# A two-layer graph network on 64 graphs: the order of work at both ends, and the engine of one sum of spectra

## The chip, the cores and the metric

The kernel runs on one core of a Trainium2 chip. Its time is in device microseconds, and the figure for a kernel is the median of its runs. The kernel before has three: 2018.05, 2020.08 and 2021.51 us, median 2020.08.

The engines are named as in the profile: PE is the matrix engine (TensorE) and PEld its loads of weights, DVE is VectorE, ACT is ScalarE, POOL is GpSimd, and SP is the engine that issues most of the DMAs. All times are in microseconds; L12 is line 12 of the kernel before, unless the text says otherwise.

## The reference

The inputs are x and adj, both 64 graphs x 256 x 256 in float32. Cut to what matters here, `reference()` computes:

```python
# layer 0
deg = adj.sum(-1); deg = where(deg != 0, deg, 1)
a_plus = deg**-.5 * adj * deg**-.5 + max(alpha, 1e-10) * eye(256)
x = layernorm(x + (a_plus @ x) @ W.T + b)
# layer 1
h = relu(bn1(conv1(x)))                   # 1x1 convolution, 256 -> 256
x_conv = relu(bn2(conv2(h)) + x)          # 17 taps, 256 -> 256
s = x @ w_se.T + b_se                     # 3 numbers for each node
A = exp(-squared_distances(s)) * adj
x_nmp = A @ relu(x @ w_msg.T + b_msg)
gi = concat(x_conv, x_nmp) @ w_ih.T + b_ih; gh = x @ w_hh.T + b_hh
r, z = sigmoid(gi_r + gh_r), sigmoid(gi_z + gh_z)
out = layernorm(x + (1 - z) * tanh(gi_n + r * gh_n) + z * x)
```

## The kernel before, in words

**The whole.** Everything is in float32. The 64 graphs are worked in four quarters of 16. The convolution with 17 taps is done through a small Fourier transform along the nodes: the forward transform of each graph's h is p_dft (L538), the products with the spectra of the weights are p_k (L605), once a quarter for its 16 graphs, and the gates are p_g (L950), which take the largest part of PE's time. The spectra of the weights are made in 13 parts (`weights(n)`, NPARTS = 13), each beside one of the first graphs.

**What sets the order.** Each stage is a Python generator that yields between its pieces, and the code that interleaves them puts the pieces in a written order. A scheduler then orders the instructions of each engine; `tc.issue_after(op)` keeps an instruction from standing ahead of `op` in that order. Within an engine, instructions run in their order, so one that waits holds all behind it. GpSimd, SP and ACT also issue DMAs, in the same queues as their other work.

**Layer 0 of a graph g** (`layer0(g)`): ACT sums the rows of adj to degrees (L402); GpSimd raises them to the power -0.5 (`dis`, L412, named POWERS[g]); PE transposes adj in four blocks (p_adjT, L423); ACT copies the blocks to adjT; VectorE adds the diagonal, one L426 for each half (DIAGONAL[g]); ACT scales x by `dis` (L441, X_SCALED[g]); GpSimd adds the bias to x (L444, 128x512); PE makes p_hT (L449, 8 products); ACT copies it to hT (L454); PE makes p_out (in the bank p_out0, L459, 8 products); VectorE adds x to it (L464, two). The layer norm follows: statistics on VectorE (L355 to L357), a power on GpSimd (L358), the mean's product on VectorE (L362), and the scaling on ACT (L366, two). ACT then issues the store of x1 (L470).

**Layer 1 of a graph**, as far as it is spoken of here: PE transposes x1 (p_x1T, L484), does conv1 and the three columns of s together (p_conv, L499), the messages (p_msg, L520), the transform (p_dft, L538), the rows for the distances (p_rows, L551), the distances (p_dist, L561) and the aggregation (p_nmp, L574). VectorE squares the columns of s (`sq`, L509; L511 and L512 write `scols`, which p_rows reads). ACT relus the messages (L524).

**The first microseconds.** Two graphs (`firsts`) go through layer 0 beside the setup. SP's queue holds, in order, adj and x of graph 0, adj of graph 1, small vectors, x of graph 1 and weights. `batch_norms()` transposes the vectors of both batch norms (p_bn, L181), makes six diagonal matrices on VectorE (into VM, L195), and multiplies them by a matrix of ones (p_norm, L200) so that each vector stands in all 128 rows; these scale conv1 (wc, L204 and L207) and the taps. `without_first()` (L155) is a GpSimd subtraction of a row from a weight: once for wc, once for wmsg. `tables()` writes a period of a cosine (memsets, L234), copies 30 strided rows of it into `fwd_row` on VectorE (15 at L252, 15 at L253), loads six slices of it into `fwd` (L263, on SP), then loads x of graph 2, makes `w_row` on VectorE (L269 to L274), loads it as `wt` (L280, L281) and from it makes the matrix `dft_w` (L288).

**A part of the spectra** (`weights(n)`): six loads of taps for the next part; products p_u (L332) of dft_w with the taps for i = 0 and 1, and copies of them on ACT (L335); after the second, VectorE scales the next part's taps (L316, for part 0 before all this); then VectorE takes the difference of the two spectra (L341, 120x1024), GpSimd their sum (L342, 120x1024), and GpSimd issues three stores `ud` (L344).

**The end.** `gru(63)` works its 128 top rows and its 128 lower rows apart, and the top rows in two halves of columns. After the products, `mixed()` makes tanh's input (L1007 to L1013), the gated x (L1016) and calls tanh; `rest()` (L927, L928) finishes a piece; `finished()` and `ended()` run `normed()`, a layer norm and a store (L921) issued by ACT. The top rows' second half of columns comes last:

```python
        mixed(top, slice(1, 2))
        nc.vector.bn_stats(st[:, 1, :], y[:, 0, HD:])
        NORMS.append(normed(g, top, y, st))
        ended()
```

Of the kernel before, what the change touches and what calls it, by code (L numbers as in the profile page):

```python
# [14 lines left out]
P = 128  # L15
# [11 lines left out]
def kernel(  # L27
# [100 lines left out]
    neg_half = const.tile([P, 4], F32)  # L128
    nc.vector.memset(neg_half, -0.5)
    load(0)  # L130
    nc.scalar.dma_start(alpha_t, bcast_rows(alpha, 1))
# [44 lines left out]
    def batch_norms(pool):  # L176


        scale = pool.tile([P, D], F32, name="scale")
        p = bank("p_bn")  # L180
        nc.tensor.transpose(p[:, :16], vectors, ident[:16, :16])  # L181
        cols = pool.tile([P, 4, 4], F32, name="bn")
        nc.vector.tensor_copy(cols.rearrange("p i n -> p (i n)"), p[:, :16])
        g, b, m, v = (cols[:, i, :] for i in range(4))
        nc.vector.tensor_scalar(v, v, BN_EPS, None, op0=ALU.add)
        nc.gpsimd.tensor_tensor(v, v, neg_half, op=ALU.pow)
        ones = pool.tile([P, P], F32, name="ones")
        nc.vector.memset(ones, 1.0)
# [41 lines left out]
    def tables(pool):  # L230
# [18 lines left out]
        for n, f in enumerate(FREQ):  # L249

            if f < 0 or f % 3 == 0:
                nc.vector.tensor_copy(fwd_row[:, :, RE[n]], wave(f, False, FL))  # L252
                nc.vector.tensor_copy(fwd_row[:, :, IM[n]], wave(-f, True, FL))  # L253
# [38 lines left out]

    TAPS_OF, NORMALISED, STATISTICS = {}, [], []

# [23 lines left out]
    def weights(pool, n, scale):  # L318
# [4 lines left out]
        if n == 0:  # L323
            scaled(tp, scale)
        m = NU * GC
# [14 lines left out]
        with tc.issue_after(ADEG[n + 3]), tc.issue_after(POWERS[n + 3]):  # L340
            nc.vector.tensor_sub(us[3], us[1], us[0])  # L341
            nc.gpsimd.tensor_tensor(us[2], us[0], us[1], op=ALU.add)  # L342
# [4 lines left out]
    def layernorm(y, eps=LN_EPS, normed=None, parts=None, first=None):  # L347

# [12 lines left out]
        with tc.issue_after(ADEG[first]) if first in ADEG else ExitStack():  # L361
            nc.vector.scalar_tensor_tensor(mr[:, : len(chunks)], mv[:, : len(chunks), 0], -1.0, rs[:, : len(chunks)], op0=ALU.mult, op1=ALU.mult)  # L362
        if normed is not None:
            yield
        for c in chunks:
            op = nc.scalar.activation(  # L366
# [21 lines left out]
    EVICTED, RELU, SQUARED, AGGREGATED, LAYER0, POWERS = {}, {}, {}, {}, {}, {}  # L388
    ADJT, X1, X_SCALED, DIAGONAL, ADEG = {}, {}, {}, {}, {}


    def layer0(g):
# [13 lines left out]

        at = X_SCALED[0] if g == 1 else AGGREGATED.get(g - 3)
        with tc.issue_after(at) if at else ExitStack():
# [25 lines left out]

        if g > 1:
            yield
# [6 lines left out]
        with tc.issue_after(POWERS[max(g, 1)]):  # L443
            nc.gpsimd.tensor_tensor(x_t, x_t, b0_t.unsqueeze(1).to_broadcast([P, NCH, D]), op=ALU.add)  # L444
        hT = work.tile([P, DCH, N], F32, name="hT", bufs=1)
        p = bank("p_hT").rearrange("p (k n) -> p k n", k=DCH)
        for k in range(DCH):
            for mc in range(NCH):
                nc.tensor.matmul(  # L449
                    p[:, k, :], x1[:, mc, k * P : (k + 1) * P],  # L450
                    adjT[:, mc, 1 - mc : 3 - mc, :].rearrange("p n q -> p (n q)"),
                    start=mc == 0, stop=mc == NCH - 1,
                )
        nc.scalar.copy(hT, p)  # L454
        yield
        p = bank("p_out0").rearrange("p (c o) -> p c o", c=NCH)
        for c in range(NCH):
            for k in range(DCH):
                nc.tensor.matmul(  # L459
                    p[:, c, :], hT[:, k, c * P : (c + 1) * P], w0[:, k, :], start=k == 0, stop=k == DCH - 1  # L460
                )
        for c in range(NCH):
            mark(
# [454 lines left out]
    def normed(g, part, y, parts=None):  # L918

        yield from layernorm(y, 4 * LN_EPS, None, parts)  # L920
        nc.scalar.dma_start(out[g].rearrange("(c p) d -> p c d", p=P)[:, part], y)  # L921

    REST = []

    def rest():
        z, i, yq = REST.pop()
        nc.vector.scalar_tensor_tensor(i, z, 1.0, i, op0=ALU.subtract, op1=ALU.mult)  # L927
        nc.vector.tensor_sub(yq, yq, i)  # L928

# [4 lines left out]
    def gru(g):  # L934
# [68 lines left out]
        def mixed(part, cols=slice(0, 2)):  # L1003
# [8 lines left out]
            )  # L1012
            nc.vector.scalar_tensor_tensor(i, n, 0.5, i, op0=ALU.mult, op1=ALU.add)  # L1013
            y = x1[:, part]
# [20 lines left out]

        top = slice(0, 1)
        squashed(0, top)
# [114 lines left out]
    with tc.tile_pool(name="setup", bufs=1) as setup:  # L1152
# [236 lines left out]
```

## Time and profile before

| | before |
|---|---|
| median of 3 runs | 2020.08 (2018.05 to 2021.51) |
| the profiled execution's own time | 2018.59 |
| its span | 2016.8 |
| its mean granted TensorE clock | 0.997 |
| PE busy | 1977.2 (98%), 8169 matmuls |
| DVE busy | 1396.2 (69%), 3221 instructions |
| ACT busy | 970.4 (48%), 2310 instructions |
| POOL busy | 681.2 (34%), 651 instructions |
| HBM | 147 GB/s over the span |

The profile is of one execution, whose span starts with its first instruction and ends with its last; the time of that execution is 1.79 longer than its span. The slices that the page prints are 50.4 us each, so the first slice holds the setup, both first graphs and the start of the third. In a row of the timeline the first number is the start, the second how long the row's instructions took together from the first to the end of the last, and x8 how many they are; in brackets stands the idle time of the engine just ahead, and what ended it. A row of the windows has the stretch's length, then busy time and count of PE, of its weight loads, of DVE, ACT and POOL, then the granted clock, the busy share of the DMA engines, and GB/s.

### The profile page before, as it was taken

Reading aid. Unit: us, or ns where it says so; the run is one execution under the profiler, and the core shown is the slowest. Engines: PE = TensorE matmul, PEld = TensorE weight load, DVE = VectorE, ACT = ScalarE, POOL = GpSimd, SP = SyncE. Lnnn points to the kernel's source line nnn. Section 1 sums busy time; section 2 is a strip of 40 time slices with the busy share of each in tenths; the row PEclk is TensorE's granted clock in tenths of the full one; section 3 lists DMA queues with packets and bytes.
Section 4 is the critical chain, followed back from the end, with each engine's and each line's share of the span. In section 5 each row is a group of like instructions: output and inputs, shape, how many; then the busy total and the mean of one; then the engine's idle time right before and its main releaser. Section 6 shows DMA issues by size and latency. Waiting matters only on the chain.

```text
span 2016.8 us, 26474 instructions
## 1 busy us (share of the span) xinstructions
PE 1977.2 (98%) x8169; PEld 1439.2 (71%) x8169; DVE 1396.2 (69%) x3221; ACT 970.4 (48%) x2310; POOL 681.2 (34%) x651
## 2 busy tenths in 40 slices
PE   7999999999999999999999999999999999999998
PEld 6888788878677766777777766778878655555554
DVE  6344448787567788764446888874338899788887
ACT  5766654567442234566653233557762233333333
POOL 4444411132433243223322234231230344444543
PEclk9999999999999999999999999999999999999999
DMA  4676657544546744343335665434229554534331
GB/s 135 207 224 214 199 191 241 167 137 132 140 136 212 215 125 133 115 136 110 105 105 182 210 182 139 123 105 141 100 71 301 156 141 126 131 90 103 96 92 58
DMA packets 256803, 298.88 MB, mean 148 GB/s; under 512 B 70470, under 2 KB 199116, under 8 KB 256662
## 3 DMA queue, kind: packets, MB, share of 16 engines
q1 hardware_dynamic: 195798, 200.39, 33.7%
q10 hardware_dynamic: 44480, 67.39, 9.4%
q0 software_dynamic: 16384, 29.40, 6.5%
q8 instruction: 67, 1.10, 0.2%
q14 instruction: 74, 0.61, 0.1%
HBM read 193.97 MB, written 103.08 MB: 147 GB/s over the span
## 4 chain that ended last, share of the span: by engine, by line
PE 83%; DVE 11%; ACT 2%; issue 1%; DMA 1%; POOL 1%; ACTq 0%; POOLq 0%; DVEq 0%
PE p_g L950 36%; PE p_k L605 11%; PE p_hT L449 5%; PE p_out L459 5%; PE p_nmp L574 5%; PE p_conv L499 4%; PE p_msg L520 4%; PE p_dft L538 4%; PE p_u L332 2%; PE p_dist L561 2%; PE p_x1T L479 2%; PE p_adjT L423 1%; DMA u<-ud 1%; DVE ln_st L355 1%; PE p_xcT L898 1%
## 5 line engine op out<-in xcount | busy, mean ns | idle before, releaser
L950 PE MATMUL p_g<-wall,sums 128*128 128x384 f32 x1536 | 532.8, 487 | 1.7 <-DVE G L982 1.7
L950 PEld LDWEIGHTS p_g<-wall,sums 128*128 128x128 f32 x1536 | 285.4, 190 | 187.7 <-issue 8.2
L950 PE MATMUL p_g<-wall,inputs 128*128 128x384 f32 x1152 | 406.0, 488 | 3.7 <-DVE G L972 3.5
L950 PEld LDWEIGHTS p_g<-wall,inputs 128*128 128x128 f32 x1152 | 216.2, 190 | 156.5 <-DVE G L972 15.7
L358 POOL TENSOR_TENSOR ln_rs<-ln_rs,neg_half 128x2 f32<-128x2 f32 x129 | 97.1, 753 | 566.8 <-DVE ln_rs L357 430.2
L914 POOL TENSOR_TENSOR sums<-inputs 128x384 f32<-128x384 f32 x128 | 150.2, 1173 | 261.9 <-PE p_g L950 235.2
L565 DVE TENSOR_TENSOR aT<-aT,adjT 128x512 f32<-128x512 f32 x64 | 44.5, 696 | 202.6 <-ACT aT L562 202.4
L605 PE MATMUL p_k<-u,VM 128*128 128x256 f32 x736 | 169.8, 380 | 2.6 <-DMA u<-ud 1.4
L444 POOL TENSOR_TENSOR x_t<-x_t,b_t 128x512 f32<-128x512 f32 x64 | 101.9, 1592 | 204.9 <-ACT x L441 111.2
L605 PEld LDWEIGHTS p_k<-u,VM 128*128 128x128 f32 x736 | 138.9, 190 | 24.8 <-ACT ab L651 3.6
L366 ACT ACTIVATE x_g<-x_g,ln_mr,ln_rs 128x256 f32<-128x256 f32 x128 | 70.0, 593 | 156.8 <-DVE ln_mr L362 155.4
L1001 ACT ACTIVATE G<-G 128x512 f32<-128x512 f32 (+1 forms) x129 | 81.0, 628 | 125.9 <-DVE G L1030 87.7
L449 PE MATMUL p_hT<-adjT,x 128*128 128x256 f32 x512 | 125.2, 388 | 5.8 <-ACT x L441 2.6
L499 PE MATMUL p_conv<-wc,xn 128*128 128x259 f32 x512 | 124.8, 386 | 0.7 <-issue 0.7
L574 PE MATMUL p_nmp<-aT,msg 128*128 128x256 f32 x512 | 121.3, 380 | 1.9 <-DVE aT L565 1.9
L459 PE MATMUL p_out<-w,hT 128*128 128x256 f32 x512 | 121.4, 380 | 0.9 <-ACT hT L454 0.7
L974 ACT COPY G<-p_g 128x512 f32<-128x512 f32 x64 | 37.4, 585 | 174.4 <-PE p_g L950 116.2
L520 PE MATMUL p_msg<-wmsg,xn 128*128 128x256 f32 x512 | 121.3, 379 | 0.0
L914 POOL TENSOR_TENSOR sums<-inputs,sums 128x384 f32<-128x384 f32 x64 | 72.6, 1134 | 137.6 <-PE p_g L950 137.5
L538 PE MATMUL p_dft<-fwd,h 128*128 128x240 f32 x512 | 114.1, 366 | 0.0
L499 PEld LDWEIGHTS p_conv<-wc,xn 128*128 128x128 f32 x512 | 98.1, 192 | 21.3 <-issue 1.1
L449 PEld LDWEIGHTS p_hT<-adjT,x 128*128 128x128 f32 x512 | 93.9, 193 | 22.9 <-ACT x L441 7.1
(174 smaller groups left out, 3582.7 us busy)
## 6 DMA issues: line engine op xcount, KB each, us to landing
u<-ud SPq DMA_DIRECT2D x284, 256.0 KB
xn_d<-xn ACTq DMA_DIRECT2D x64, 512.0 KB
inputs<-xn_d SPq DMA_DIRECT2D x64, 512.0 KB
ud<-u_set POOLq DMA_DIRECT2D x39, 480.0 KB, 6.1
adj_t<-in_adj_dram SPq DMA_DIRECT2D x64, 256.0 KB
x_t<-in_x_dram SPq DMA_DIRECT2D x64, 256.0 KB
x_d<-x ACTq DMA_DIRECT2D x64, 256.0 KB
xc_d<-VM SPq DMA_DIRECT2D x64, 256.0 KB
```

What stands on the lines that cost most here:

```text
L358: nc.gpsimd.tensor_tensor(rs[:, : len(chunks)], rs[:, : len(chunks)], neg_half[:, : len(chunks)], op=ALU.pow)
L444: nc.gpsimd.tensor_tensor(x_t, x_t, b0_t.unsqueeze(1).to_broadcast([P, NCH, D]), op=ALU.add)
L449: nc.tensor.matmul(p[:, k, :], x1[:, mc, k * P : (k + 1) * P], adjT[:, mc, 1 - mc : 3 - mc, :].rearrange("p n q -> p (n q)"), start=mc == ...
L459: nc.tensor.matmul(p[:, c, :], hT[:, k, c * P : (c + 1) * P], w0[:, k, :], start=k == 0, stop=k == DCH - 1)
L499: CONV1[g] = nc.tensor.matmul(p, x1T[:, k, c * P : (c + 1) * P], wc1[:, k, :], start=k == 0, stop=k == DCH - 1).ins
L520: nc.tensor.matmul(p[:, c, :], x1T[:, k, c * P : (c + 1) * P], wmsg[:, k, :], start=k == 0, stop=k == DCH - 1)
L538: nc.tensor.matmul(p[:, t0 * FL : t1 * FL], h[:, c, k * P : (k + 1) * P], fwd[:, first : first + t1 - t0, :].rearrange("p t f -> p (t f)") ...
L574: nc.tensor.matmul(p[:, k, :], msg[:, mc, k * P : (k + 1) * P], aT[:, mc].rearrange("p n q -> p (n q)"), start=mc == 0, stop=mc == NCH - 1,)
L605: nc.tensor.matmul(p[:, j * D : (j + 1) * D], v[:, k, :], u[:, k, :], start=k == 0 and j == 0 and not onto, stop=k == DCH - 1, skip_group_ ...
L914: nc.gpsimd.tensor_tensor(S[i], x, y, op=op)
L950: nc.tensor.matmul(p[:, : 3 * HD] if k == 0 else p[:, HD:], a[:, k], wall[:, b, k].rearrange("p t d -> p (t d)"), start=first and k == 0, ...
L1001: nc.scalar.activation(rz, rz, AF.Tanh, scale=0.5)
```

## The change

- A matrix of ones is made first of all, and `awake(9)` issues nine 128x128 products of it with itself ahead of the first load's line; one more stands after the transposes of each of the two first graphs. Nothing reads their results.
- The two first graphs and `batch_norms` go in another order: hT of graph 0, out0 of graph 0, hT of graph 1, the norms' products p_norm, out0 of graph 1. New names (HT, OUT0, AGGREGATE, BIASED, MEANS) carry the constraints between them. The subtraction of wc stands behind the bias sum of graph 1's x.
- The 15 copies L253 go from VectorE to ACT, behind the scaled x of graph 1. The two operations that complete `fwd_row` stand behind the first statistics. Of SP's loads, x of graph 2 goes ahead of the six of `fwd`. The first part's taps are scaled behind graph 0's normalised x. The degrees of graph 2 stand behind it too.
- The last part's sum of spectra (L342 for n = 12) goes from GpSimd to VectorE.
- At the end the lower rows' layer norm is tied behind the top rows' tanh input (MIXED) and the rest of the norms behind the last finished piece (RESTED). The top rows' final scaling is split: the left half of the columns on ACT, the right half on VectorE, and two stores, the right half's by SP and the left half's by ACT.

```diff
+    ones = const.tile([P, P], F32, name="ones")
+    nc.vector.memset(ones, 1.0)
+    def awake(times):
+        p = bank("p_awake")
+        for _ in range(times):
+            nc.tensor.matmul(p[:, :P], ones, ones, start=True, stop=True)
+    awake(9)
     load(0)
...
             if f < 0 or f % 3 == 0:
                 nc.vector.tensor_copy(fwd_row[:, :, RE[n]], wave(f, False, FL))
-                nc.vector.tensor_copy(fwd_row[:, :, IM[n]], wave(-f, True, FL))
+        behind_diagonal.close()
+        yield
+        with tc.issue_after(X_SCALED[1]):
+            for n, f in enumerate(FREQ):
+                if f < 0 or f % 3 == 0:
+                    nc.scalar.copy(fwd_row[:, :, IM[n]], wave(-f, True, FL))
+        yield
+        behind_diagonal.enter_context(tc.issue_after(STATISTICS[0]))
...
         behind_diagonal.close()
+        load_x(2)
         for j in range(GT // 2 + 2):
             ...
             nc.sync.dma_start(fwd[lo:hi, j, :], fwd_row[:, lo - first : hi - first])
-        load_x(2)
...
         if n == 0:
-            scaled(tp, scale)
+            with tc.issue_after(NORMALISED[0]):
+                scaled(tp, scale)
...
-            nc.gpsimd.tensor_tensor(us[2], us[0], us[1], op=ALU.add)
+            (nc.gpsimd if n + 1 < NPARTS else nc.vector).tensor_tensor(us[2], us[0], us[1], op=ALU.add)
...
+        if halved:
+            nc.vector.tensor_scalar(
+                y[:, 0, D // 2 :], y[:, 0, D // 2 :], rs[:, 0:1], mr[:, 0:1], op0=ALU.mult, op1=ALU.add
+            )
+            nc.scalar.activation(
+                y[:, 0, : D // 2], y[:, 0, : D // 2], AF.Identity, bias=mr[:, 0:1], scale=rs[:, 0:1]
+            )
+            return
...
-        at = X_SCALED[0] if g == 1 else AGGREGATED.get(g - 3)
+        at = X_SCALED[0] if g == 1 else NORMED[0] if g == 2 else AGGREGATED.get(g - 3)
...
-        if g > 1:
+        if g > 0:
             yield
...
+            nc.sync.dma_start(to[:, :, HD:], y[:, :, HD:])
+            nc.scalar.dma_start(to[:, :, :HD], y[:, :, :HD])
...
-        finished(slice(1, 2), mixed(slice(1, 2)))
+        y1 = mixed(lower)
         nc.vector.tensor_add(quarter(0, 1), quarter(0, 1), p5)
-        squashed(0, slice(1, 2))
-        mixed(top, slice(1, 2))
+        squashed(0, lower)
+        mixed(top, lower)
+        with tc.issue_after(MIXED[0]):
+            finished(lower, y1)
         nc.vector.bn_stats(st[:, 1, :], y[:, 0, HD:])
-        NORMS.append(normed(g, top, y, st))
-        ended()
+        with tc.issue_after(RESTED[0]):
+            ended()
+        run(normed(g, top, y, st))
...
         for stage in firsts:
             next(stage)
+            awake(1)
         next(norms)
-        with tc.issue_after(POWERS[1]):
-            without_first(wc1, top[:, : D + NSE], nc.gpsimd)
-            nc.gpsimd.tensor_copy(wc1[0:1, 0, D:], biases[:, :NSE])
         load_adj(2)
         fill = tables(setup)
         next(fill)
-        for stage in firsts:
-            next(stage)
-        run(take(firsts[0], 2))
-        with tc.issue_after(STATISTICS[0]):
+        next(firsts[0])
+        with tc.issue_after(HT[0]):
             next(firsts[1])
+        next(fill)
+        next(firsts[0])
+        with tc.issue_after(OUT0[0]):
+            next(firsts[1])
+        with tc.issue_after(BIASED[1]):
+            without_first(wc1, top[:, : D + NSE], nc.gpsimd)
+            nc.gpsimd.tensor_copy(wc1[0:1, 0, D:], biases[:, :NSE])
+        with tc.issue_after(AGGREGATE[1]):
+            next(norms)
+        next(firsts[0])
+        next(fill)
+        run(firsts[0])
+        with tc.issue_after(MEANS[0]), tc.issue_after(HT[1]):
             scale2 = next(norms)
-        run(firsts[0])
+            next(firsts[1])
         run(fill)
```

More of the change, by code (lines that the diff above doesn't have):

```diff
@@ L186, in batch_norms @@
         nc.gpsimd.tensor_tensor(v, v, neg_half, op=ALU.pow)
-        ones = pool.tile([P, P], F32, name="ones")
-        nc.vector.memset(ones, 1.0)
         with tc.issue_after(DIAGONAL[1]):
@@ L252, in tables @@
                 nc.vector.tensor_copy(fwd_row[:, :, RE[n]], wave(f, False, FL))
-                nc.vector.tensor_copy(fwd_row[:, :, IM[n]], wave(-f, True, FL))
+        behind_diagonal.close()
[4 more added lines that the diff above has]
+                    nc.scalar.copy(fwd_row[:, :, IM[n]], wave(-f, True, FL))
+        yield
+        behind_diagonal.enter_context(tc.issue_after(STATISTICS[0]))
         parts = fwd_row[:, :, 16:].rearrange("p t (h n) -> p t h n", h=2)
@@ L291, in tables @@
         )
-    TAPS_OF, NORMALISED, STATISTICS = {}, [], []
+    TAPS_OF, NORMALISED, STATISTICS, MEANS = {}, [], [], {}
     def load_taps(pool, n):
@@ L345, in weights, with layernorm @@
         yield
-    def layernorm(y, eps=LN_EPS, normed=None, parts=None, first=None):
+    def layernorm(y, eps=LN_EPS, normed=None, parts=None, first=None, halved=False):
         chunks = range(y.shape[1])
@@ L361, in layernorm @@
         with tc.issue_after(ADEG[first]) if first in ADEG else ExitStack():
-            nc.vector.scalar_tensor_tensor(mr[:, : len(chunks)], mv[:, : len(chunks), 0], -1.0, rs[:, : len(chunks)], op0=ALU.mult, op1=ALU.mult)
+            mean = nc.vector.scalar_tensor_tensor(mr[:, : len(chunks)], mv[:, : len(chunks), 0], -1.0, rs[:, : len(chunks)], op0=ALU.mult, op1=ALU.mult)
+        MEANS.setdefault(0, mean.ins)
         if normed is not None:
             yield
+        if halved:
[6 more added lines that the diff above has]
+            return
         for c in chunks:
@@ L388 @@
     EVICTED, RELU, SQUARED, AGGREGATED, LAYER0, POWERS = {}, {}, {}, {}, {}, {}
-    ADJT, X1, X_SCALED, DIAGONAL, ADEG = {}, {}, {}, {}, {}
+    ADJT, X1, X_SCALED, DIAGONAL, ADEG, BIASED, HT, AGGREGATE, OUT0 = {}, {}, {}, {}, {}, {}, {}, {}, {}
     def layer0(g):
@@ L443, in layer0 @@
         with tc.issue_after(POWERS[max(g, 1)]):
-            nc.gpsimd.tensor_tensor(x_t, x_t, b0_t.unsqueeze(1).to_broadcast([P, NCH, D]), op=ALU.add)
+            BIASED[g] = nc.gpsimd.tensor_tensor(x_t, x_t, b0_t.unsqueeze(1).to_broadcast([P, NCH, D]), op=ALU.add).ins
         hT = work.tile([P, DCH, N], F32, name="hT", bufs=1)
@@ L448, in layer0 @@
             for mc in range(NCH):
-                nc.tensor.matmul(
+                AGGREGATE[g] = nc.tensor.matmul(
                     p[:, k, :], x1[:, mc, k * P : (k + 1) * P],
@@ L452, in layer0 @@
                     start=mc == 0, stop=mc == NCH - 1,
-                )
-        nc.scalar.copy(hT, p)
+                ).ins
+        HT[g] = nc.scalar.copy(hT, p).ins
         yield
@@ L458, in layer0 @@
             for k in range(DCH):
-                nc.tensor.matmul(
+                out0 = nc.tensor.matmul(
                     p[:, c, :], hT[:, k, c * P : (c + 1) * P], w0[:, k, :], start=k == 0, stop=k == DCH - 1
                 )
+        OUT0[g] = out0.ins
         for c in range(NCH):
@@ L918, in normed @@
     def normed(g, part, y, parts=None):
-        yield from layernorm(y, 4 * LN_EPS, None, parts)
-        nc.scalar.dma_start(out[g].rearrange("(c p) d -> p c d", p=P)[:, part], y)
-    REST = []
+        yield from layernorm(y, 4 * LN_EPS, None, parts, halved=parts is not None)
+        to = out[g].rearrange("(c p) d -> p c d", p=P)[:, part]
+        if parts is None:
+            nc.scalar.dma_start(to, y)
+        else:
+            nc.sync.dma_start(to[:, :, HD:], y[:, :, HD:])
+            nc.scalar.dma_start(to[:, :, :HD], y[:, :, :HD])
+    REST, MIXED, RESTED = [], {}, {}
     def rest():
@@ L927, in rest @@
         nc.vector.scalar_tensor_tensor(i, z, 1.0, i, op0=ALU.subtract, op1=ALU.mult)
-        nc.vector.tensor_sub(yq, yq, i)
+        RESTED[0] = nc.vector.tensor_sub(yq, yq, i).ins
     def ended():
@@ L1012, in mixed @@
             )
-            nc.vector.scalar_tensor_tensor(i, n, 0.5, i, op0=ALU.mult, op1=ALU.add)
+            MIXED[0] = nc.vector.scalar_tensor_tensor(i, n, 0.5, i, op0=ALU.mult, op1=ALU.add).ins
             y = x1[:, part]
@@ L1034, in gru @@
             return
-        top = slice(0, 1)
+        top, lower = slice(0, 1), slice(1, 2)
         squashed(0, top)
```

## The prediction

> **What bounds the kernel now.** I read the page first: where PE is not full, and who is on the chain that ended last.
>
> ```profile
> PE   7999999999999999999999999999999999999998
> ...
> PE 83%; DVE 11%; ACT 2%; issue 1%; DMA 1%; POOL 1%; ACTq 0%; POOLq 0%; DVEq 0%
> ```
>
> PE is the bound in every slice but the first and the last. An edit gains only where PE waits, or where it runs at half clock. So I went through the timeline of the first 34 us.
>
> ```profile
> 7.89 6.15 PE L449 MATMUL p_hT<-adjT,x 128*128 128x256 f32 x16
> ...
> 14.01 1.19 POOL L155 TENSOR_TENSOR wc<-wc,top 128x518 f32<-128x518 f32 x1 [3.88 <-DMA taps<-in_conv2T_dram]
> 14.04 1.22 DVE L252 COPY fwd_row<-period 1x48 f32<-1x48 f32 x1
> 15.16 1.26 POOL L444 TENSOR_TENSOR x_t<-x_t,b_t 128x512 f32<-128x512 f32 x1
> 15.18 1.31 DVE L253 COPY fwd_row<-period 1x48 f32<-1x48 f32 x1
> ...
> 21.47 1.27 POOL L155 TENSOR_TENSOR wmsg<-wmsg,top 128x512 f32<-128x512 f32 x1
> 22.00 0.75 DVE L362 SCALAR_TENSOR_TENSOR ln_mr<-ln_mv,ln_rs 128x2 f32<-128x2 f32 x1
> 22.79 1.09 ACT L366 ACTIVATE x<-x,ln_mr,ln_rs 128x256 f32<-128x256 f32 x2 [2.53 <-DVE ln_mr L362]
> ...
> 25.53 3.79 PE L499 MATMUL p_conv<-wc,xn 128*128 128x259 f32 x8 [0.70 <-issue]
> ...
> 33.52 1.89 PE L449 MATMUL p_hT<-adjT,x 128*128 128x256 f32 x8
> ```
>
> From p_conv at 25.53 PE is dense. A copy of 48 numbers normally follows the last by 0.11 us, but takes 1.2 to 1.3 beside a large GpSimd sum and ends with it; the 128x2 product L362 (0.15 elsewhere) is held to the end of the wmsg sum. One long GpSimd sum stops VectorE. Next the windows, for the clock:
>
> ```profile
> 19.70:23.10 3.40, 0.13 (x2) 0.00 (x0) 3.37 (x11) 0.70 (x2) 2.26 (x3) 1.00 0.06 8
> 23.10:26.50 3.40, 2.34 (x6) 1.52 (x7) 3.40 (x21) 2.87 (x9) 0.27 (x2) 0.50 0.48 121
> 26.50:29.90 3.40, 3.40 (x11) 2.69 (x10) 0.25 (x3) 0.98 (x5) 1.18 (x2) 0.50 0.16 47
> ...
> 2006.20:2009.60 3.40, 1.18 (x4) 0.38 (x2) 3.16 (x10) 1.46 (x3) 0.00 (x0) 1.00 0.24 80
> 2009.70:2013.00 3.30, 0.00 (x0) 0.00 (x0) 2.10 (x11) 0.91 (x2) 1.20 (x2) 0.50 0.01 3
> ```
>
> Second column: busy PE; third from the end: granted clock. The clock steps every 3.4 us: half after a stretch with 0.13 us of PE, full again after a full one, half after one with only 1.18. Before the first step no clock is recorded, but p_hT's 16 records in 6.15 us, against 8 in 1.89 later, show half speed at the start too. Last, graph 12, whose weights part is the last of 13:
>
> ```profile
> 233.81 2.96 POOL L342 TENSOR_TENSOR u_set<-u_set,u_set 120x1024 f32<-120x1024 f32 x1
> 234.49 2.31 DVE L509 SCALAR_TENSOR_TENSOR sq<-scols 128x6 f32<-128x6 f32 x1
> 237.11 2.69 DVE L426 SCALAR_TENSOR_TENSOR adjT<-ident,adeg,adjT 128x128 f32<-128x128 f32 x2
> 237.44 0.41 PE L551 MATMUL p_rows<-ident,scols 128*128 128x128 f32 x2 [0.56 <-DVE scols L512]
> 239.95 1.53 PE L449 MATMUL p_hT<-adjT,x 128*128 128x256 f32 x6 [1.67 <-DVE adjT L426]
> ```
>
> The GpSimd sum of spectra holds L509, the next x_t sum holds L426, and PE stands still. By the starts of its products (p_rows 0.72 after p_dft could hand over, p_hT 1.83) that is 2.55 us.
>
> **The change, part by part** (line numbers of before).
>
> Last sum on VectorE: the GpSimd sum of 2.96 goes; VectorE does it in about 1.21 (L341, same shape). By the new order: L341 233.35 to 234.56, L509 to 234.7, the sum to 235.85, L511, L426, L512 and L426 (0.16, 0.35, 0.26, 0.35, overlapping) to 236.65. PE wants p_rows at 236.72 and p_hT at 236.94; the x_t sum cannot start before ACT's scaled x at 236.69. So 2.5 comes back. If x_t's sum catches the second L426 first, 1.27 is lost again: bounds 1.2 to 2.55.
>
> First graph. GpSimd now does x_t's first bias sum ahead of wc's subtraction, from about 10.2 (the second `dis`, 9.44 + 0.70), to 11.5. That falls on VectorE's diagonals L195, which ran free at 10.24 to 11.6; one or two slip by, the next waits. GpSimd then waits for bn2_bias (`less_one`), does the second x_t sum at 12.7 to 14.0, and wc's subtraction at 14.0 to 15.2 as before, its load being the same. Both hold VectorE, so most of the 15 copies L252 run from 15.25: 15 x 0.114 = 1.7, to 17.0. (At half clock in hT the second sum is at 13.3 and the copies end at 17.1: the products of ones, nine of 0.43 at half clock = 3.8 us from 1.1, fill PE's wait for adj at 4.97 and cost nothing, but decide little.) L464 on x of graph 0 at 17.0 and 17.4, against 19.15 for the second one before; from there to the end of L357 was 1.55, so 18.95; L358 0.08 + 0.72, to 19.75; the wmsg sum directly behind it, 1.27, to 21.0, holds L362 as it did. ACT's L366 starts at 21.03 instead of 22.79: 1.75 gained. p_conv came 2.75 later: 23.8.
>
> Clock. From p_conv to p_hT of graph 2 the chain's own pieces give 1.75 + 0.44 + 1.73 + 1.62 + 0.22 = 5.76 at full clock; it took 7.99, so 2.2 went to the half clock. Now PE's last products before p_conv are p_out0 of graph 1, behind L464 at 17.9 to 19.8, and only the transposes at 21.7 stand in the 4 us to 23.8. The row of 2006.20 says that a third of a window does not hold the clock, so it falls about 22 to 25 and returns one full window (3.41) later: 1.0 to 2.7 lost, taken as 1.8. That is 0.4 gained. The Trainium skill, "TensorE: Matmul & The Clock Gate", Part 1, lets the clock fall only after an idle window; by it the first graph would stay at full clock and gain some 1.4 more, to 2014.5. The row at 2006.20, one third busy and then half clock, is against it.
>
> The gain has a cap. Graph 1's L464 comes behind wc (0.67 + 0.40) and w_row (1.2), at 23.3; 0.87 + 0.73 + taps 1.20 + 0.3 for statistics, two GpSimd powers of 0.70, L362: 28.1; then ACT: two L366 1.1, msg 0.6, scaled x 0.5 with issue between: p_hT of graph 2 not before 30.7, 2.8 before the 33.52 of now. Start: -2.1, bounds -0.5 and -2.8.
>
> Moved at no cost: 15 copies on ACT (its 128x4 copy 0.19, 1x256 0.36: about 3 us) in the 3.57 us it idled before the second hT; behind them waits that hT copy, and p_out0, which waits for L464 at 17.9 anyway. Uncovered they would cost 0.4. SP takes x of graph 2 at 17.5 instead of 23.74; the six `fwd` loads still start at 19.4 (19.29 before), and the last now stands behind the landing of ACT's x1 store. Behind it queue six `wt`, adj, x and seven `taps`. The store goes out at 22.2; the last output's, issued at 2013.87, had landed by 2015.61, so SP goes on at some 25, `fwd` is there at 27.7, p_dft comes at 29.4. Two spare ones products (0.43) lie in PE's waits for adj and bn.
>
> Graph 1. The first product of part 1 (p_u) moves from the adjT transposes into the middle of p_dft; taps' scaling L316 moves from 42.28 to behind L341 (44.36 to 45.58). There GpSimd's sum is already waiting (44.95) and takes over, as at 233.81: to 47.80. L316, two SBUF inputs, 1.22: to 49.05. PE is at p_u after conv, adjT, msg and half of p_dft: 43.38 + 1.75 + 0.44 + 1.73 + 0.81 = 48.1. So +1.0; zero if L316 wins the port, 1.2 at most.
>
> End. The operations left ahead of L1013, tanh's input, are 0.12 shorter in sum, so it comes that much sooner; but the lower rows' L362 now stands ahead of the top's aggregate and waits for GpSimd at 2011.8, so the top's mean is known at 13.15 instead of 13.2.
>
> ```profile
> 2013.24 0.60 ACT L366 ACTIVATE x_g<-x_g,ln_mr,ln_rs 128x256 f32<-128x256 f32 x1 [1.18 <-DVE ln_mr L362]
> 2013.87 0.35 ACTq L921 DMA_DIRECT2D out_dram<-x_g  x1
> ```
>
> Half of the row on ACT ends at 13.67 (0.48), the store of the lower rows is issued first (0.37), so the last store starts at 14.1, not 13.87: +0.2; bounds -0.2 (smaller store) and +0.5 (three stores at once).
>
> Sum: -2.1 - 2.5 + 1.0 + 0.2 = -3.4. The profiled execution took 2018.59 (span 2016.8): 2015.2. The median of the runs, 2020.08, lies 1.5 above that execution; half of it is added, since four executions spread over 3.5 us: 2015.9, that is 0.21% under the median. About 0.2% is what a measurement of this kernel can tell from no change; the border lies at 2016.0.
>
> **Rivals.** *Ports lie more kindly*: VectorE gets the pair between sums, L316 does not wait, the start reaches its cap: -2.8 - 2.5 + 0 + 0.2 = -5.1, 2014.2. For it: at 16.40 copies got through between two sums. Against: every L342 that met waiting work won.
>
> *Part of it comes back*: x_t's sum holds L426 at graph 12 (-1.2) and the start gives 0.8: -0.8 - 1.2 + 1.0 + 0.2 = -0.8, 2018.5. For it: 1.5 us of start are three estimates long.
>
> *Slower*: SP behind the x1 store. From a landing later than 26.6 p_dft waits (29.4 less issue and landing, 2.7) us for us; past 34 the loss passes 3.4 + 4 and the kernel is slower by over 0.2%, some 2025. Against it: 1.74 for a store in the row above.
>
> *It does not do what it says*: nine products do not raise the clock before hT. Then hT of graph 0 stays at 3.8 us; by the working above this moves L464 by 0.1, 2016.0. It is counted in the first case.
>
> **How the numbers follow.** Forecast 0.45 (own range 2014.6 to 2017.4, somewhat over half of it under 2016.0, 0.27), kind ports 0.18, part comes back 0.25, slower 0.12. Faster 0.27 + 0.18 = 0.45; same 0.18 + 0.25 = 0.43; slower 0.12. The range takes in the first three with their bounds: 2012.2 to 2019.9.
>
> **What would show it.** L464 of graph 0 at 17, L366 at 21, p_conv at 23.5 to 24, half clock beside it; p_hT of graph 2 at 31 to 32; a wait of p_u for L316 near 46; no waits of p_rows and p_hT near 233; the last store 0.2 later after the last p_g. A p_conv before 22 or a full clock there, or p_u without a wait, makes the forecast too high; a p_dft that waits for `fwd` makes it wrong.

## The result, and the profile after

| | before | after |
|---|---|---|
| median of 11 runs each | 2019.39 (2018.05 to 2021.66) | 2015.05 (2013.57 to 2017.72) |
| ratio | | 0.9978, 95% interval 0.9971 to 0.9986 |
| the profiled execution's own time, its span | 2018.59, 2016.8 | 2015.05, 2013.3 |

The kernel became faster by 0.22%, from 2019.39 to 2015.05; 2015.9 was predicted. Line numbers of the kernel after differ: L252 and L253 are L261 and L267, L441 is L467, L444 is L470, L464 is now L491, L362 is L379, L366 is L392, L499 is L526, L449 is L475, L332 is L349 (p_u), L316 is L332 (taps), L341 and L342 are L358 and L359, L155 is L165. From the page of after:

```profile
PE   8999999999999999999999999999999999999998
...
PE 81%; DVE 12%; ACT 2%; DMA 2%; issue 1%; POOL 1%; SPq 0%; ACTq 0%; POOLq 0%; DVEq 0%
```

The first slice has risen from 7 to 8 tenths, and no other slice of this row has moved. To see where the time went, products that both kernels make are set side by side, by their starts in the two traces:

| start of | before | after | shift |
|---|---|---|---|
| first p_conv | 25.53 | 22.98 | -2.55 |
| p_hT of graph 2 | 33.52 | 30.34 | -3.18 |
| p_hT of graph 3 | 50.86 | 48.61 | -2.25 |
| p_hT of graph 4 | 67.81 | 66.15 | -1.66 |
| p_hT of graph 14 | 224.34 | 222.68 | -1.66 |
| p_hT of graph 16 | 253.02 | 248.06 | -4.97 |
| last p_nmp | 1508.79 | 1504.30 | -4.49 |
| last p_g group | 1999.47 | 1996.33 | -3.14 |
| end of the span | 2016.81 | 2013.28 | -3.53 |

The steps between neighbouring rows are the terms of the sum: start -3.18, graph 1 +0.93, graph 2 +0.59, graph 13 and what follows it -3.31, and the end -0.39. (The last part of the spectra falls beside graph 13; the prediction called it graph 12.) Between graph 16 and the last p_g lies +1.83, where the two kernels run the same instructions in the same order.

Rows picked from the timeline of after, in the first 60 us:

```profile
7.94 1.99 PE L475 MATMUL p_hT<-adjT,x 128*128 128x256 f32 x8
11.89 1.32 POOL L470 TENSOR_TENSOR x_t<-x_t,b_t 128x512 f32<-128x512 f32 x1 [1.55 <-DMA b_t<-in_b_dram]
11.90 4.74 DVE L261 COPY fwd_row<-period 1x48 f32<-1x48 f32 x12
19.27 1.27 POOL L165 TENSOR_TENSOR wmsg<-wmsg,top 128x512 f32<-128x512 f32 x1
19.34 1.22 DVE L379 SCALAR_TENSOR_TENSOR ln_mr<-ln_mv,ln_rs 128x2 f32<-128x2 f32 x1 [0.35 <-POOL ln_rs L375]
20.59 1.09 ACT L392 ACTIVATE x<-x,ln_mr,ln_rs 128x256 f32<-128x256 f32 x2 [5.09 <-DVE ln_mr L379]
22.98 2.07 PE L526 MATMUL p_conv<-wc,xn 128*128 128x259 f32 x4 [0.70 <-issue]
30.34 1.89 PE L475 MATMUL p_hT<-adjT,x 128*128 128x256 f32 x8
...
41.75 2.87 POOL L359 TENSOR_TENSOR u_set<-u_set,u_set 120x1024 f32<-120x1024 f32 x1
42.32 3.38 DVE L332 TENSOR_TENSOR taps<-taps,scale 85x1024 f32<-85x1024 f32 x1
45.75 1.99 PE L349 MATMUL p_u<-taps,dft_w 85*120 85x256 f32 x8 [0.67 <-DVE taps L332]
...
56.01 1.20 DVE L332 TENSOR_TENSOR taps<-taps,scale 85x1024 f32<-85x1024 f32 x1
57.27 3.28 PE L349 MATMUL p_u<-taps,dft_w 85*120 85x256 f32 x14 [0.33 <-DVE taps L332]
```

hT of graph 0 now runs at full speed (1.99). Twelve copies, which follow each other by some 0.11 when nothing holds them, still take 4.74 among the GpSimd sums (the first of three is shown), and the wmsg sum still holds the 128x2 product to its own end. Beside graph 1 the scaling of taps takes 3.38 instead of 1.22: the sum of spectra runs from 41.75 to 44.62, and the scaling ends 1.08 later, close to the forecast; PE waits for it in p_u. Beside graph 2 the scaling takes its usual 1.20 but stands behind the first statistics (at 56.01; in before it came at 54.90, ahead of L464), and PE waits again. The clock, by windows of one step each:

```profile
15.84:19.25 3.41, 1.71 (x8) 1.44 (x8) 3.12 (x15) 0.00 (x0) 1.03 (x3) 1.00 0.64 174
19.26:22.66 3.40, 1.12 (x6) 0.45 (x4) 3.29 (x16) 1.70 (x4) 1.67 (x3) 1.00 0.19 56
22.67:26.08 3.41, 3.10 (x8) 2.51 (x9) 3.28 (x11) 1.63 (x7) 0.34 (x1) 0.50 0.31 86
```

1.71 us of PE in a step kept the clock, 1.12 did not, and one step with 3.10 at half clock brought it back. Beside graph 13, and after it:

```profile
232.90 1.21 DVE L359 TENSOR_TENSOR u_set<-u_set,u_set 120x1024 f32<-120x1024 f32 x1
235.06 0.38 PE L578 MATMUL p_rows<-ident,scols 128*128 128x128 f32 x2
235.27 1.89 PE L475 MATMUL p_hT<-adjT,x 128*128 128x256 f32 x8
...
248.06 1.99 PE L475 MATMUL p_hT<-adjT,x 128*128 128x256 f32 x8 [0.46 <-ACT x L467]
```

The sum takes 1.21 on VectorE, neither product waits any more, and the next p_hT waits 0.46 instead of the 0.81 of before:

```profile
253.02 1.99 PE L449 MATMUL p_hT<-adjT,x 128*128 128x256 f32 x8 [0.81 <-ACT x L441]
```

The end:

```profile
2008.81 0.60 ACT L392 ACTIVATE x_g<-x_g,ln_mr,ln_rs 128x256 f32<-128x256 f32 x1 [1.57 <-DVE ln_mr L379]
...
2009.74 0.16 DVE L379 SCALAR_TENSOR_TENSOR ln_mr<-ln_mv,ln_rs 128x1 f32<-128x1 f32 x1 [0.66 <-POOL ln_rs L375]
2009.94 0.49 ACT L387 ACTIVATE x_g<-x_g,ln_mr,ln_rs 128x128 f32<-128x128 f32 x1 [0.53 <-DVE ln_mr L379]
...
2009.94 0.35 ACTq L950 DMA_DIRECT2D out_dram<-x_g  x1
2010.31 0.35 SPq L952 DMA_DIRECT2D out_dram<-x_g  x1
2010.46 0.35 ACTq L953 DMA_DIRECT2D out_dram<-x_g  x1
```

The lower rows were scaled by 2009.41, but ACT issues their store (L950) only at 2009.94, when the top's half has started: the store does not stand ahead of that half.

### The profile page after: what moved, and what is told of

It is laid out like the page before. It is cut to its first block, busy times and chain, and to the rows that moved or that the text cites. A ratio compares the mean times of both kernels' runs of the same rounds, so it can differ in the third digit from the quotient of the medians.

```text
span 2013.3 us, 26520 instructions
## 1 busy us (share of the span) xinstructions
PE 1978.1 (98%) x8191; PEld 1440.6 (72%) x8191; DVE 1394.0 (69%) x3208; ACT 972.3 (48%) x2325; POOL 678.7 (34%) x650
## 4 chain that ended last, share of the span: by engine, by line
PE 81%; DVE 12%; ACT 2%; DMA 2%; issue 1%; POOL 1%; SPq 0%; ACTq 0%; POOLq 0%; DVEq 0%
PE p_g L982 34%; PE p_k L632 11%; PE p_hT L475 5%; PE p_out L485 5%; PE p_nmp L601 5%; PE p_conv L526 4%; PE p_msg L547 4%; PE p_dft L565 4%; PE p_u L349 2%; PE p_dist L588 2%; PE p_x1T L506 1%; PE p_adjT L449 1%; DVE VM L686 1%; DVE ln_st L372 1%; DVE VM L687 1%
## 5 line engine op out<-in xcount | busy, mean ns | idle before, releaser
L470 POOL TENSOR_TENSOR x_t<-x_t,b_t 128x512 f32<-128x512 f32 x64 | 101.8, 1590 | 204.9 <-ACT x L467 106.4
L392 ACT ACTIVATE x_g<-x_g,ln_mr,ln_rs 128x256 f32<-128x256 f32 x127 | 69.4, 593 | 158.7 <-DVE ln_mr L379 157.3
L475 PE MATMUL p_hT<-adjT,x 128*128 128x256 f32 x512 | 122.7, 382 | 3.8 <-ACT x L467 2.2
L526 PE MATMUL p_conv<-wc,xn 128*128 128x259 f32 x512 | 124.5, 384 | 0.7 <-issue 0.7
L526 PEld LDWEIGHTS p_conv<-wc,xn 128*128 128x128 f32 x512 | 97.8, 192 | 20.9 <-issue 0.9
L485 PEld LDWEIGHTS p_out<-w,hT 128*128 128x128 f32 x512 | 95.0, 190 | 21.1 <-ACT hT L480 2.4
```

The costliest lines, as they stand in the source:

```text
L470: BIASED[g] = nc.gpsimd.tensor_tensor(x_t, x_t, b0_t.unsqueeze(1).to_broadcast([P, NCH, D]), op=ALU.add).ins
L475: AGGREGATE[g] = nc.tensor.matmul(p[:, k, :], x1[:, mc, k * P : (k + 1) * P], adjT[:, mc, 1 - mc : 3 - mc, :].rearrange("p n q -> p (n q)" ...
L485: out0 = nc.tensor.matmul(p[:, c, :], hT[:, k, c * P : (c + 1) * P], w0[:, k, :], start=k == 0, stop=k == DCH - 1)
L526: CONV1[g] = nc.tensor.matmul(p, x1T[:, k, c * P : (c + 1) * P], wc1[:, k, :], start=k == 0, stop=k == DCH - 1).ins
```

## The experiments

The theory: each gain and loss lies where the table puts it, and one long GpSimd sum stops VectorE. The rivals are named run by run. One microsecond is 0.05% of the time, so single terms are read from the traces' stages, and the times only judge sums of them. A stage is known no better than two executions agree: with the same code at the start, p_conv to p_hT of graph 2 took 7.99 in before, 7.66 in sum_only and 8.68 in end_only, as the steps of the clock fell differently. Starts in us:

| run | first p_conv | p_hT of graph 2 | of graph 4 | graph 14 to 16, shift | time |
|---|---|---|---|---|---|
| after | 22.98 | 30.34 | 66.15 | -3.31 | 0.9978 (0.9971 to 0.9986) |
| sum_only | 25.63 | 33.30 | 67.59 | -3.02 | 0.9988 (0.9979 to 0.9997) |
| end_only | 25.30 | 33.99 | 68.28 | -0.03 | 1.0001 (0.9992 to 1.001) |
| all_sums | 22.89 | 30.41 | 65.29 | -3.31 | 0.9971 (0.9959 to 0.9983) |
| no_awake | 22.82 | 31.61 | 67.50 | -3.31 | 0.9982 (0.9973 to 0.9991) |
| no_awake2 | 20.79 | 29.01 | 65.00 | -3.30 | 0.9988 (0.9979 to 0.9997) |
| copies_back | 24.79 | 33.16 | 69.03 | -3.31 | 2017.38, one run |
| scaled_late | 22.93 | 30.45 | 66.25 | -3.31 | 2016.45, one run |
| keep_clock | 23.48 | 29.32 | 63.70 | -3.30 | 2012.36, one run |
| noawake_keep | 23.53 | 29.85 | 64.24 | -3.31 | 2012.68, one run |
| wmsg_dve | 21.84 | 28.35 | 64.25 | -3.00 | 2015.87, one run |
| three | 23.50 | 29.34 | 63.63 | -3.31 | 0.9964 (0.9952 to 0.9976) |
| best | 22.30 | 28.13 | 62.42 | -2.95 | 0.9959 (0.9945 to 0.9972) |

**sum_only**, the kernel before with one edit:

```diff
-            nc.gpsimd.tensor_tensor(us[2], us[0], us[1], op=ALU.add)
+            (nc.gpsimd if n + 1 < NPARTS else nc.vector).tensor_tensor(us[2], us[0], us[1], op=ALU.add)
```

> Only the last part's sum of spectra goes from GpSimd to VectorE; all else as before. The prediction's step: up to p_hT of graph 4 nothing moves (within 0.1 us), no waits of PE beside graph 13 (0.56 and 1.67 before), 2.5 us gained there; 2016.1 against the profiled 2018.59, ratio 0.9988. The profile after says more: 3.3, since p_hT of the next graph also waits less (0.46 for 0.81), so 2015.3, ratio 0.9984. Rival, the gain there hangs on the earlier start of the changed kernel: 1.5 or less, ratio over 0.9992.

Measured: -0.21 up to p_hT of graph 14 (all of it is there by p_hT of graph 2, from the clock's steps), then -3.02 within two graphs, ratio 0.9988, 2016.49. The edit stands by itself; it does not need the earlier start. The forecast -2.5 was the waits beside graph 13 alone; what the next graph regains was missing.

**end_only**: the kernel before with the diff's edits of `layernorm`, `normed`, `rest`, `mixed` and the last lines of `gru`.

> Only the end is rearranged (lower rows' norm, halves, two stores); all else as before. The prediction's step: last store issued 0.2 us later after the last p_g, ratio 1.0001. The profile after shows the opposite: from the last copy of p_g on VectorE to the last store's issue 5.72 us against 5.99, and 0.4 less from the last p_g to the end of the span: ratio 0.9998. Both lie under what the times can tell; the profile decides between +0.2 and -0.3.

From VectorE's last sum with p_g (L1056, 2010.65) to the last store's issue (2016.37) it is 5.72, as after, against 5.99; the last p_g to the end of the span gains 0.36. The rearranged end is a gain of a third of a microsecond, not a loss of 0.2. Of the twelve traces with this end eleven gain 0.35 to 0.39; in that of best the store is issued after 5.72 too, but what follows it takes some 0.4 longer than in after.

**all_sums**, the kernel after with every sum of spectra on VectorE:

```diff
-            (nc.gpsimd if n + 1 < NPARTS else nc.vector).tensor_tensor(us[2], us[0], us[1], op=ALU.add)
+            nc.vector.tensor_tensor(us[2], us[0], us[1], op=ALU.add)
```

> The changed kernel with all 13 sums of spectra on VectorE instead of the last alone. Theory (a waiting GpSimd sum takes VectorE's place for its whole length): the scaling of taps beside graph 1 takes 1.2 us instead of 3.38 and ends by 44.9, and p_u's wait of 0.67 there goes: p_hT of graph 3 0.8 us earlier than in the changed kernel, 47.8. Graph 2's wait of p_u (0.33) is one of order on VectorE and stays. From graph 3 to 12 nothing moves, as PE does not wait there. Ratio to the kernel before 0.9974. Rival: 1.2 us more on VectorE for each part makes its other work late, and PE waits in the graphs 3 to 12: p_hT of graph 14 later than 222.7, ratio 0.998 or more.

The scaling beside graph 1 takes 1.21 (42.38), p_u follows without a wait, and p_hT of graph 3 comes at 47.75. Graph 2's wait of 0.33 stays, and from graph 4 to 14 nothing moves. So the 0.93 of graph 1 needs the GpSimd sum.

**no_awake** and **no_awake2**, the kernel after without `awake(9)` and both `awake(1)`, twice:

> The changed kernel without the products of ones (all eleven left out). The prediction's step: hT of graph 0 falls back to half clock (3.8 to 6.2 us instead of 2.0), but the VectorE sum for graph 0 comes only 0.1 later, so p_conv within 0.2 of 22.98 and p_hT of graph 2 within 0.3 of 30.34; ratio to the kernel before 0.998, as with them. Rival: the early clock is what the start gains by: p_conv at 24 or later, p_hT of graph 2 over 31.3, ratio 0.9985 or more.

> The changed kernel without its eleven products of ones, once more, for another execution's profile. The clock's steps are 3.41 us apart in every profile, but where they lie against the start of the span differs from one execution to the next (first rise 4.2 to 6.9 us with the products, 11.8 to 14.0 without). Theory of the phase: what the half clock costs beside the first p_conv hangs on where a step happens to end, not on the products: this execution's phase differs from 11.76, the step at half clock ends after one step (p_hT of graph 2 near 30.3) or does not come at all (near 29), unless the phase is again near 11.8, and the ratio over all runs is that of the changed kernel, 0.9978 within 0.0005. Rival, the products themselves bring it: two steps at half clock whatever the phase, p_hT of graph 2 at 31.6, ratio 0.9984.

In the first, p_conv came 0.16 sooner than after, and yet p_hT of graph 2 came 1.27 later. The windows of no_awake say why:

```profile
18.59:21.99 3.40, 1.50 (x8) 0.77 (x6) 3.02 (x13) 1.36 (x3) 2.17 (x3) 1.00 0.27 81
22.00:25.41 3.41, 2.71 (x8) 2.14 (x7) 3.41 (x14) 2.54 (x9) 0.00 (x0) 0.50 0.29 83
25.42:28.82 3.40, 3.40 (x11) 2.74 (x11) 1.22 (x10) 1.39 (x4) 1.37 (x2) 0.50 0.06 12
```

The step ended at 22.00 instead of 22.67, so p_conv filled only 2.71 us of the next, and the clock stayed at half for a second step. In no_awake2 it never fell: p_conv came at 20.79, for a reason that bears on the theory:

```profile
18.20 0.16 DVE L378 SCALAR_TENSOR_TENSOR ln_mr<-ln_mv,ln_rs 128x2 f32<-128x2 f32 x1 [0.35 <-POOL ln_rs L374]
...
20.67 1.27 POOL L164 TENSOR_TENSOR wmsg<-wmsg,top 128x512 f32<-128x512 f32 x1 [2.50 <-DMA top<-in_w_msgT_dram]
```

The load for wmsg landed late, the GpSimd sum came after the mean product, and that took 0.16 instead of 1.22. So the phase theory's forecast that another execution need not show two steps held, though here the earlier p_conv helped, and the phase was not the only thing that differed. Its ratio (0.9978 within 0.0005) was not met: 0.9988. Over both sets the median without the products is 2015.96 (21 runs) against 2015.05 (11 runs). The products seem worth some 0.9, not 0.1, but the intervals of the ratios overlap, so this is not shown. 0.43 of it is seen in both traces without them: beside graph 2 p_u waits 0.77 instead of 0.33, as VectorE's order differs. The rest may be the clock's steps; noawake_keep below bears on it.

**copies_back**, the 15 copies on VectorE behind the diagonals of graph 1:

```diff
-        with tc.issue_after(X_SCALED[1]):
+        with tc.issue_after(DIAGONAL[1]):
...
-                    nc.scalar.copy(fwd_row[:, :, IM[n]], wave(-f, True, FL))
+                    nc.vector.tensor_copy(fwd_row[:, :, IM[n]], wave(-f, True, FL))
```

> The changed kernel with its 15 copies of the cosine's sine rows back on VectorE, behind the diagonals of graph 1, instead of on ACT. The prediction called their move free on ACT; what it is worth on VectorE: 15 of 0.114, 1.7 us ahead of graph 0's sum of x and p_out, 16.54 to 18.2; p_conv 22.98 to 24.7, p_hT of graph 2 30.34 to 32.0. If they ride between the GpSimd sums, under 0.5 of it.

The 15 copies ran from 16.34 to 18.09, the sum of x and p_out at 17.99, p_conv at 24.79 as expected. p_hT of graph 2 lost 2.82, not 1.7: the step from 16.30 to 19.70 held only 0.70 us of PE, and the clock stayed at half until 29.94. The move to ACT is a main part of the start's gain: without it 0.36 of the 3.18 is left in this trace. What the new order of the first graphs' products gains by itself, no run isolates.

**scaled_late** and **keep_clock**: the first scaling of taps behind graph 1's mean, and eight products of ones in PE's wait ahead of the first p_x1T.

```diff
-        MEANS.setdefault(0, mean.ins)
+        MEANS.setdefault(len(MEANS), mean.ins)
...
-            with tc.issue_after(NORMALISED[0]):
+            with tc.issue_after(MEANS[1]):
                 scaled(tp, scale)
```

```diff
         p = bank("p_x1T").rearrange("p (k n) -> p k n", k=DCH)
+        for _ in range(8 if g == 0 else 0):
+            nc.tensor.matmul(p[:, 0, :P], ones, ones, start=True, stop=True)
```

> The changed kernel with the first part's scaling of taps (1.22 us, beside the first p_conv) put behind graph 1's mean instead of behind wc. Graph 1's mean product then comes 1.0 earlier than 27.14, but PE is at half clock and dense up to p_hT of graph 2: that stays at 30.34, within 0.1 (cap theory: two caps, clock and layer norm, and removing one brings little). Rival, the layer norm alone sets it: 29.3.

> The changed kernel with eight more products of ones (0.87 us) in PE's wait ahead of the first p_x1T. In the changed kernel the clock fell at 22.67, after a step of 3.41 us with 1.13 us of PE in it; the step before had 1.72 and held it. Now that step has 2.0. Theory of the cap (graph 1's layer norm on ACT is next in line): full clock from p_conv on, but p_hT of graph 2 only 0.45 earlier than the 30.34 of the changed kernel, 29.9. Rival, the half clock alone sets it: 1.6 earlier, 28.7. Rival, 2.0 of 3.41 does not hold the clock: 30.3, half clock as before. Only the stages up to there are compared: the order of p_u beside graph 1 moves too.

scaled_late moved p_hT of graph 2 by +0.11: PE at half clock sets it. keep_clock had full clock from 4.2 us until 2004.43, when PE had run dry; the step with p_x1T:

```profile
21.30:24.70 3.40, 1.90 (x10) 1.41 (x10) 3.28 (x22) 2.56 (x10) 0.42 (x1) 1.00 0.32 87
```

From p_conv to p_hT of graph 2 it now took 5.84, against 5.76 worked out for full clock in the prediction, and 7.36 after. p_conv itself came 0.5 later, because ACT did the degrees of graph 2 ahead of xn. At 29.32, it lies between the two forecasts: the cap by graph 1's norm that I expected at 29.9 was not there yet. Beside graphs 1 and 2 the order on VectorE changed as a side effect: the scaling of taps now stands ahead of the spectra's difference and ahead of graph 4's sum, as in the kernel before.

```profile
39.59 1.22 DVE L332 TENSOR_TENSOR taps<-taps,scale 85x1024 f32<-85x1024 f32 x1
...
41.89 1.89 PE L349 MATMUL p_u<-taps,dft_w 85*120 85x256 f32 x8
```

No p_u waits beside either graph, though all sums but the last are still on GpSimd. So the 0.59 comes from VectorE's order, and the 0.93 needs both, the changed order and a sum on GpSimd that gets in ahead of the scaling.

**noawake_keep**: both edits together, no `awake`, and the eight products.

> The changed kernel without its eleven products of ones, but with eight in PE's wait ahead of the first p_x1T, as in keep_clock. Without the eleven p_hT of graph 2 came 1.27 later than in the changed kernel although p_conv came 0.16 sooner, with the clock at half for two steps (22.0 to 28.8) instead of one. Theory: the eleven are worth their effect on the steps of the clock and nothing else; with the clock held by the eight, leaving them out costs nothing: full clock from p_conv on, p_hT of graph 2 within 0.3 of the 29.31 of keep_clock. Rival: the two microseconds that hT of graph 0 takes longer pass on to p_conv: p_hT of graph 2 at 30.3 or later.

Full clock from 11.8 us on, p_hT of graph 2 at 29.85: 0.53 later than keep_clock, where no_awake was 1.27 later than after. In no_awake PE had no wait on the way, so the 1.27 there was the clock's; holding the clock brings back 0.7 of it. The other 0.5 is lost again, 0.31 of it as a wait of p_hT for ACT's scaled x; why that comes later is not explained. Neither forecast (within 0.3, or 30.3) was met.

**wmsg_dve**, the kernel after with the wmsg sum on VectorE:

```diff
-        without_first(wmsg, top[:, D + NSE :], nc.gpsimd)
-        nc.gpsimd.tensor_copy(wmsg[0:1, 0], biases[:, NSE:])
+        without_first(wmsg, top[:, D + NSE :], nc.vector)
+        nc.vector.tensor_copy(wmsg[0:1, 0], biases[:, NSE:])
```

> The changed kernel with the subtraction of wmsg on VectorE, behind graph 1's first statistics, instead of on GpSimd. Theory (the GpSimd sum holds graph 0's mean product L379: 1.22 where 0.15 is normal): that product takes 0.15 to 0.2, x1 of graph 0 is scaled 1.1 sooner, p_conv at 21.9 instead of 22.98. Graph 1's own norm then waits for the subtraction on VectorE (0.9) and p_hT of graph 2 gains less: 29.4. Rival: L379 waits for something else; p_conv within 0.2 of 22.98.

```profile
19.24 0.16 DVE L379 SCALAR_TENSOR_TENSOR ln_mr<-ln_mv,ln_rs 128x2 f32<-128x2 f32 x1 [0.34 <-POOL ln_rs L375]
...
21.84 1.11 PE L526 MATMUL p_conv<-wc,xn 128*128 128x259 f32 x4 [0.70 <-issue]
```

p_conv came 1.14 sooner, as expected. With it, a step of the clock held 2.69 us of PE and kept it full, so p_hT of graph 2 gained 1.99, more than forecast. The time of its one run, 2015.87, does not show the gain: this execution lost 1.98 against before between p_hT of graph 16 and the last p_nmp, in the same code.

**three** joins keep_clock, scaled_late and all_sums. **best** adds wmsg_dve and puts graph 2's degrees behind ACT's second copy of graph 0's p_x1T.

> The changed kernel with three edits at once: eight products of ones ahead of the first p_x1T, the first scaling of taps behind graph 1's mean, and all 13 sums of spectra on VectorE. In its order the scaling of taps stands ahead of the difference of spectra beside graph 1, and ahead of graph 4's sum of x and p_out beside graph 2. Cap theory: with both caps gone p_hT of graph 2 comes 1.4 earlier, 28.9; no wait of p_u beside graphs 1 and 2 (0.83 and 0.59 in the changed kernel), so p_hT of graph 4 is 2.8 earlier than its 66.15 there: 63.3; ratio to the kernel before 0.9964. Rival: another wait (wt, fwd or taps not landed) takes the first 1.4, ratio 0.9971 as for all_sums.

> The kernel of the run three with the subtraction of wmsg on VectorE and the degrees of graph 2 behind the copies of graph 0's x1T on ACT, which they had overtaken there (0.5 us). Theory: p_conv at 21.9 instead of 23.50, full clock throughout, p_hT of graph 2 at 28.0 instead of 29.34 (graph 1's norm, with the subtraction ahead of it, is next in line), p_hT of graph 4 at 62.3 instead of 63.63; ratio to the kernel before 0.9958. Rival: the tables (fwd, wt) are not there 1.3 sooner and p_dft or p_u waits: ratio 0.9964 as before these two edits.

three: p_hT of graph 2 at 29.34 (28.9 expected; the degrees cost 0.5), no wait of p_u, ratio 0.9964 as expected. best: 28.13 and 62.42, against 28.0 and 62.3 expected; median 2010.66, ratio 0.9959. It beats both kernels, the one after by some 4 us. What it adds to three (0.0005) is not told apart by the times; the stages show 1.2 up to graph 14, of which 0.35 is lost again by graph 16.

## Why the prediction was right or wrong

**The total.** 2015.2 was worked out for an execution, and the profiled one took 2015.05; from median to median -4.2 was forecast and -4.3 measured. That closeness is partly luck: the terms that the change touches come to -5.4 (by the table), not -3.4, and +1.83 lies where nothing was changed. Most of that, +1.35, lies after the last p_nmp. In the twelve traces of the runs above, which have the same code there, the same stretch takes from 0.18 less to 2.35 more than in the trace of before; end_only, whose code differs only at the very end, has +2.29. So the profiled execution of before seems a quick one there, and the half offset that was added for this (0.7) had the right sign. A rival is left: the two traces without the rearranged end, before and sum_only, are the two quickest of the fourteen in this stretch, and the time of end_only (1.0001) cannot tell a microsecond from none.

**Start, -2.1 with bounds -0.5 and -2.8; measured -3.18.** The mechanisms were right: sums hold the copies, the wmsg sum holds the mean, one step at half clock. The measured value lies beyond the bound. Three sizes were off: L464 of graph 0 at 16.54, not 17.0 (three copies got in ahead of the sums); from L366 to p_conv 2.39, not 2.74, as the degrees of graph 2 no longer stand wholly ahead of xn on ACT; and the half clock cost 1.6, not 1.8. The bound by graph 1's norm (30.7) was at least 0.4 too late: graph 1's L464 came at 22.71, the estimate was 23.3. The 1.4 more that the prediction gives for a full clock would have passed that bound by 0.7; keep_clock, at full clock, came 1.0 before after.

**Last sum, -2.5, upper bound -2.55; measured -3.02 alone and -3.31 in the change.** The step that failed is the bound: it counted the waits beside graph 13 and not that VectorE's lag was passed on to graph 14, where L464 came 0.62 behind p_nmp in before and 0.26 in after, and p_hT waits for ACT's scaled x.

**Graph 1, +1.0; measured +0.93**, with the scaling at 3.38 where 3.47 was forecast.

**Graph 2, not in the sum; measured +0.59.** The order of VectorE beside graph 2 had changed as well (taps behind L464 and the first statistics), and the comparison of orders was followed only through graph 1 and at the named places.

**End, +0.2 with bounds -0.2 and +0.5; measured -0.39, and -0.36 alone.** The failed step is the assumption that the lower rows' store is issued by ACT between the top's half and its store (0.37): it is issued beside that half.

**The products of ones, put at 0.1.** They seem worth more, some 0.9 by the medians; the prediction saw only that hT of graph 0 is not on the path, and not that the clock's steps and the order on VectorE move with them.

**Rivals.** The kind-ports case (2014.2) was nearer at the start and wrong on graph 1. Neither SP behind the x1 store nor the return of graph 13's loss appeared: p_dft has no wait in the first 260 us of the trace of after.

**The clock's rule.** The Trainium skill, "TensorE: Matmul & The Clock Gate", Part 1, lets the clock fall only after an idle window. Steps of about 3.41 us with 0.70, 1.12 and 1.50 us of PE in them were followed by half clock here; 1.71, 1.90 and 2.69 kept it. Half-clock steps with 2.34, 2.71 and 2.75 kept it at half, 3.10 raised it. The measurement decides: a step without any work of PE is not needed for the fall.

## What to carry to other kernels

Before costing a move, compare the order of every engine as far as it differs, not only at the places that the diff names: the 0.59 lost here came from an order two graphs further on. Where GpSimd has a long sum next to short VectorE operations on the critical path, ask who gets there first; the wmsg sum, 1.27 on GpSimd and 0.65 on VectorE, brought p_conv 1.14 sooner when it was moved, and the last sum of spectra (2.96 and 1.21) brought 3.0. Where PE must wait near a step of its clock, a few products that nobody reads can be cheaper than the half clock that follows: eight of them, 0.87 in keep_clock, where the half clock cost some 1.5.

## What the runs showed of the hardware

- The clock's steps are 3.41 us apart in every trace, but start anywhere: the first rise came at 4.2 to 6.9 us in the eight traces with the eleven products, and at 11.8 to 14.0 in those without. The Trainium skill, "TensorE: Matmul & The Clock Gate", Part 1, calls the window free-running; that agrees. What the half clock costs from p_conv to p_hT of graph 2 (0, 1.6 or 3.0 us here) thus differs between executions of one kernel.
- A VectorE product of 128x2 took 0.16 or 1.22, by whether a GpSimd sum of 1.27 started just ahead of it. The Trainium skill, "SBUF — State Buffer", section "SBUF: two separate sides", has an exclusive lock that whichever starts first holds for the whole instruction; that fits the 1.22 and the 3.38. Who starts first cannot be read off the recorded starts: in keep_clock a sum of spectra is recorded from 40.82 to 44.36, and VectorE's difference, recorded 0.11 later, still took its usual 1.21. There and at 233.81 in before the sum ends 2.2 after VectorE's difference does, so its 3.54 and 2.96 hold a wait.
- ACT issued a store of 0.35 at 2009.94 while it computed for 0.49 from 2009.94 on: the issue ran beside work that stood ahead of it. What a store costs that stands ahead of such work, no run here shows.
